# Two pairs of pieces share PSUM banks in a causal attention, and its plan is written in units

## The chip, the cores and the metric

The kernel runs on one core of a Trainium2 chip. The metric is the device time of one launch, in microseconds. It is given as the median of several runs; beside it there is one execution that was recorded by the hardware profiler, and all durations of single instructions come from that one. The core has five engines that run side by side and meet through semaphores: PE (matrix products, whose weight loads have a row of their own, PEld), DVE (vector work), ACT (activations and copies), POOL (more vector work) and SP (which issues DMAs). Products land in PSUM, which has eight banks of 128 partitions by 512 float32 numbers.

## The reference, cut to what matters

The whole program is two blocks of feed-forward, attention, feed-forward over x of 2 x 2048 tokens with 256 features, all in float32: first a mixture of experts around a full attention, then a gated recurrence around a causal attention. The change lies in the causal attention alone, which is this part of the reference:

```python
    x = x + _L1_attn_ref(_layernorm(x), w_q, w_k, w_v, w_o, rel_emb)

    # _L1_attn_ref, 16 heads of 16 features, L = 2048
    q = rotary(x @ w_q.T) / sqrt(16)
    k = rotary(x @ w_k.T)
    v = x @ w_v.T
    scores = einsum('bhqd,bhkd->bhqk', q, k)
    rel = rel_emb[clip(k_pos - q_pos, -32, 32) + 32]
    scores = where(causal, scores + einsum('bhqd,qkd->bhqk', q, rel), -1e18)
    attn = softmax(scores)
    ctx = einsum('bhqk,bhkd->bhqd', attn, v) + einsum('bhqk,qkd->bhqd', attn, rel)
    out = ctx @ w_o.T
```

The relative term differs from a constant only within 32 keys before the query. That strip, with the diagonal block of 128 keys, is the "band" of a query block: 160 columns.

## The kernel before

`attention1` works in 32 groups. A group is a batch b, a block of 512 queries (qc = 0 to 3) and four heads (g), whose four copies j = 0 to 3 sit in partitions 32j to 32j+31. A product with 32 rows uses only one quarter of PE's rows, so that the products of four heads can be in the array at once. I call these quadrant products. Transposes of bands, and most jobs, use the whole array; the products with the values (`weighted`, line 1231) use 128 rows and 32 columns, one quarter of the columns for each head.

Each group passes through two stages, which overlap with the neighbouring groups:

- **The maxima** (`largest`, line 1115). The queries come in four blocks of 128 (qb). For each query block there are the far pieces (up to 512 keys each, one product, one DVE maximum of 512 columns, line 1131) and one near piece: the band (160 columns, in one or two products) and the keys of the own block before the band (96, 224 or 352 columns for qb = 1, 2, 3). On a near piece DVE adds the band's relative scores and takes its maximum in one instruction (line 1147, followed by a small read of its accumulator), and for qb > 0 takes the maximum of the rest (line 1152). After the fourth head DVE makes the negated maximum (line 1157), and one unit later POOL adds it to the stored band (`later`, line 1161).
- **The exponentials** (`exp_band`, `exp_far`, `exp`, lines 1187 to 1229). For each block of 128 keys the scores come with keys as partitions, in one bank for each head: the bands are transposed into it (lines 1218 and 1222), the rest is a quadrant product (lines 1201 and 1208). ACT takes the exponential into `pT`. One unit later `weighted` multiplies with the values into one bank (line 1237), ACT copies that (line 644) and POOL adds it to the group's sum (line 542). The last two key blocks of a group, k0+2 and k0+3, have 256 and 128 query columns left; each takes four banks, four exponentials, four products with values, a copy and an add.

The order of all this is written out by a planner (lines 1270 to 1378). It has steps of two units; a unit has at most one piece of the maxima and one key block, and runs the bands' transposes, then the quadrant products of both (heads j and j+2 taken in turn), then `weighted` of the unit before, then jobs. For k0+3 the bands come after the maxima's products. A group has 2(qc+1) steps for either stage, `Ms` to `Me` for the maxima and `Es` to `Ee` for the exponentials; `Es` is two steps after `Me` or later. A group's maxima must also wait for one of three band tiles (`free`, from the group three before) and, on every second group, for the end of the group five before. The jobs (`at`) are all other things: keys and queries with their rotation (`rotate`), values, positions, `subtract` (which puts the maxima into the queries), `divide`, output products, and layer norms for later. The jobs of one step are dealt over its two units in halves. DMAs and copies that follow a job after some time have units of their own (`sends`).

All PSUM banks are one pool of eight that is used in turn (`bank`, line 73): a new bank is the one taken eight allocations before.

Of the kernel before, what the change touches and what calls it, by code (L numbers as in the profile page):

```python
# [42 lines left out]
def macaron_kernel(ctx: ExitStack, tc: tile.TileContext, t: dict, out: bass.AP):  # L43
# [935 lines left out]
    def attention1(norm, tail, w, relk, relv, kbias, dramp, skew):  # L979
# [4 lines left out]
        with ExitStack() as s:  # L984
# [24 lines left out]
            def rotate(xa, wa, b, qc, g):  # L1009
# [8 lines left out]
                if step < 0:  # L1018
                    nc.vector.tensor_tensor(xa, xa, cos[b, qc], ALU.mult)
                    nc.vector.tensor_tensor(xb, xb, sin[b, qc], ALU.mult)  # L1020
                    nc.vector.tensor_tensor(xa, xa, xb, ALU.add)
                else:
                    op = nc.gpsimd.tensor_tensor
                    z.later(1, op, xa, xa, cos[b, qc], ALU.mult)
                    z.later(2, op, xb, xb, sin[b, qc], ALU.mult)
                    z.later(3, op, xa, xa, xb, ALU.add)
# [80 lines left out]
            def pieces(qc):  # L1107


                far = [(qb, c) for c in range(qc) for qb in range(CPB)]  # L1110
                return far + [(qb, None) for qb in range(CPB)]
# [3 lines left out]
            def largest(t, qb, c, j):  # L1115
                b, qc, g = groups[t]
                i = qc * CPB + qb
                ps = bank()
                lhsT = q[t][rows(j), ts(qb, P)]
                m = mx[t][:, qb, j]  # L1120

                def product(cols, c, k0, n):
                    nc.tensor.matmul(  # L1123
                        ps[:, ds(cols, n)], lhsT=lhsT, rhs=kT[b, c, g][rows(j), ds(k0, n)],
                        start=True, stop=True,
                    )

                if c is not None:
                    n = min(TB, i * P - BAND - c * TB)
                    product(0, c, 0, n)  # L1130
                    nc.vector.tensor_reduce(m[:, c : c + 1], ps[:, 0:n], AX.X, ALU.max)  # L1131
                    return
                lo = 0
                if qb:
                    product(0, qc, qb * P - BAND, BW)
                    n = qb * P - BAND
                    product(BW, qc, 0, n)
                else:
                    if i:
                        product(0, qc - 1, TB - BAND, BAND)  # L1140
                    else:
                        lo = BAND
                        if j == 0:
                            nc.vector.memset(band[t][:, 0, :, 0:BAND], MASKED)
                    product(BAND, qc, 0, P)
                at_ = band[t][:, qb, j, lo:]
                nc.vector.tensor_tensor_reduce(  # L1147
                    out=at_, in0=ps[:, lo:BW], in1=at_, scale=1.0, scalar=3.0 * MASKED,
                    op0=ALU.add, op1=ALU.max, accum_out=m[:, qc : qc + 1],
                )  # L1150
                if qb:
                    nc.vector.tensor_reduce(m[:, qc + 1 : qc + 2], ps[:, ds(BW, n)], AX.X, ALU.max)
                done[t, qb] = done.get((t, qb), 0) + 1
                if done[t, qb] < J:
                    return
                mneg = z.mnegs[t % 2][:, qb]
                nc.vector.tensor_reduce(  # L1157
                    mneg[:, :, z.row(t)], mx[t][:, qb, :, 0 : qc + 1 + (qb > 0)], AX.X, ALU.max,
                    negate=True,
                )  # L1160
                z.later(
                    1, nc.gpsimd.tensor_tensor, band[t][:, qb], band[t][:, qb],
                    mneg[:, :, ds(z.row(t), 1)].to_broadcast([P, J, BW]), ALU.add,
                )
# [9 lines left out]
            def key_blocks(qc):  # L1174

                k0 = qc * CPB
                if qc == 0:
                    return [0, 1, 2, 3]
                far = list(range(k0 - 1))
                near = [k0, k0 + 1, k0 + 2, k0 - 1, k0 + 3]  # L1180
                order = []
                for k in near[:-1]:
                    order += [k] + far[:1]
                    far = far[1:]
                return order + near[-1:] + far

            def exp_bank(t, kb, j):
                if (t, kb, j) not in st:
                    st[t, kb, j] = bank()
                return st[t, kb, j]  # L1190

# [21 lines left out]
            def exp_band(t, kb, j):  # L1213
# [3 lines left out]
                if qb >= 0:  # L1217
                    nc.tensor.transpose(ps[:, ts(qb, P)], band[t][:, qb, j, BAND:], ident)  # L1218
# [7 lines left out]
            def exp(t, kb, j):  # L1226
                q0 = max(0, kb - groups[t][1] * CPB) * P
                z.pTs[t, kb, j] = wk.tile([P, TB], F32, name="pT", bufs=8)
                nc.scalar.activation(z.pTs[t, kb, j][:, q0:], st.pop((t, kb, j))[:, q0:], AF.Exp)  # L1229

            def weighted(t, kb):
                b, qc, g = groups[t]
                q0 = max(0, kb - qc * CPB) * P
                pv = bank()
                for j in range(J):
                    h = (g % 2) * J + j
                    nc.tensor.matmul(  # L1237
                        pv[rows(j), q0:],
                        lhsT=v[b, kb // CPB, g // 2][:, kb % CPB, ds(h * VW, 32)],
                        rhs=z.pTs.pop((t, kb, j))[:, q0:], start=True, stop=True,  # L1240
                    )
                z.gather(t, pv, 3, q0)
# [27 lines left out]
            Ms, Me, Es, Ee, Rs, By = ([] for _ in range(6))  # L1270
            for n, (b, qc, g) in enumerate(groups):
                size = 2 * (qc + 1)
                start = Me[-1] + 1 if n else 0
                free = Es[n - NBAND] + (4 if groups[n - NBAND][1] else 2) if n >= NBAND else -9
                start = max(start, free + 5 - size)
                if n > 5 and n % 2 == 0:
                    start = max(start, Ee[n - 5] + 5)
                Ms.append(start)
                Me.append(start + size - 1)
                By.append(max(free, start - 3))  # L1280
                start = Me[-1] + 2
# [4 lines left out]
                Rs.append(start + 5)  # L1286


            largest_at, exp_at, sends = Jobs(), Jobs(), Jobs()
            for n, (b, qc, g) in enumerate(groups):  # L1290
                for i, piece in enumerate(pieces(qc)):
                    largest_at.at(Ms[n] + i // 2, None, n, *piece)
                for i, kb in enumerate(key_blocks(qc)):
                    exp_at.at(Es[n] + i // 2, None, n, kb)
            jobs = Jobs()
            at = jobs.at
            index = {x_: n for n, x_ in enumerate(groups)}
            early = {
                n: max(Ms[n] - 10, Ee[n - 5] + 1) if n > 5 else Ms[n] - 8 for n in range(0, NG, 2)
            }  # L1300
            for n in range(NG):
                at(Me[n] + 1, z.subtract, n)
            for n in early:
                at(early[n], queries, n)
                sends.at(2 * early[n] + (2 if early[n] < 0 else 6), queries_out, n)
            for b in range(B):
                for qc in range(SB):
# [3 lines left out]
                    free = early[index[b, done_, G - 2]] + 2 if done_ is not None else f - 14  # L1311
                    at(max(f - 14, free), tables, b, qc)
                    if b or qc > 1:
                        for c in range(CPB):
                            at(f - 17 + c, z.ln_stats, b, qc, c)
                        at(f - 11, z.ln_transpose, b, qc)
                    for g in range(0, G, 2):
                        f = Ms[index[b, max(qc, 1), g]]
                        due = f - 7 if qc == 0 else f - 5 - (f < 6)
                        out_ = 2 * due + (2 if f < 6 else 6)  # L1320
                        free = 2 * Ee[index[b - 1, SB - 1, g + 1]] + 2 if b and qc else 2 * due
                        at(due, keys, b, qc, g, 2 * due < free)
                        sends.at(max(out_, free), keys_out, b, qc, g)
                    for half in range(2):
                        due = Es[index[b, max(qc, 1), 2 * half]] - 1 + (qc == 0)
                        at(due if b or qc > 1 or half else -2, vals, b, qc, half)
            for n, (b, qc, g) in enumerate(groups):
                e = early[n - n % 2]
                by = max(By[n], e + (3 if e < 0 else 4))
                at(by, by_position, n)  # L1330
                sends.at(max(2 * by + 3, 2 * (Ms[n] + 2 * qc) - 6), band_load, n)
                sends.at(2 * Me[n] + 4, band_store, n)
                sends.at(2 * Es[n] + 3, positions_load, n)
                sends.at(2 * Es[n] + 6, positions_exp, n)
                at(Rs[n] - 1, positions_T, n)
                at(Rs[n], positions, n)
                end = max(Rs[n], Ee[n] + 1)
                at(end + 1, z.divide, n, b, qc, g, False)
                if g == G - 1:
                    at(end + 2, z.outputs_T, b, qc)  # L1340
                    at(end + 3, z.outputs, b, qc, 0)
                    at(end + 4, z.outputs, b, qc, 1)

            for step, fn, *args in tail:
                at(Me[-1] + step, fn, *args)
            ready = []
            for step in range(min(jobs), max(jobs) + 1):
                exps = [a for _, a in exp_at.get(step, ())]
                maxs = [a for _, a in largest_at.get(step, ())]
                todo = jobs.get(step, [])  # L1350
                for n in range(2):
                    z.begin(2 * step + n)
                    sends.run(2 * step + n)
                    e = exps[n] if n < len(exps) else None
                    m = maxs[n] if n < len(maxs) else None
                    qb = e[1] - groups[e[0]][1] * CPB if e is not None else -2
                    if -1 <= qb < CPB - 1:
                        for j in range(J):
                            exp_band(*e, j)
# [242 lines left out]
```

## Time and profile before

| | |
|---|---|
| median of three runs | 4071.13 us (4068.05 to 4072.09) |
| the profiled execution | 4068.88 us, of which its span is 4067.0 us |
| mean granted PE clock | 0.993 |
| causal attention, first rotation to last output product | about 2578 to 3874 us of the span |
| PE busy in that stage (2700 to 3800 us) | 98% to 100% of each 100 us |
| DVE and ACT there | 62% to 77%, 58% to 76% |

The profiled time is the span and 1.9 us around it, and it lies 2.3 us under the median. A PE row is called busy from the first to the last of overlapping products, so the share says that PE seldom stood empty, not that it was used well. One product in float32 is two PE records, one transpose is one. A record's listed time holds the latency of the array; how fast records follow one another is read from their starts.

### The profile page before, as it was taken

Reading aid. Unit: us, or ns where it says so; the run is one execution under the profiler, and the core shown is the slowest. Engines: PE = TensorE matmul, PEld = TensorE weight load, DVE = VectorE, ACT = ScalarE, POOL = GpSimd, SP = SyncE. Lnnn points to the kernel's source line nnn. Section 1 sums busy time; section 2 is a strip of 40 time slices with the busy share of each in tenths; the row PEclk is TensorE's granted clock in tenths of the full one; section 3 lists DMA queues with packets and bytes.
Section 4 is the critical chain, followed back from the end, with each engine's and each line's share of the span. In section 5 each row is a group of like instructions: output and inputs, shape, how many; then the busy total and the mean of one; then the engine's idle time right before and its main releaser. Section 6 shows DMA issues by size and latency. Waiting matters only on the chain.

```text
span 4067.0 us, 76436 instructions
## 1 busy us (share of the span) xinstructions
PE 3996.5 (98%) x28256; PEld 1930.7 (47%) x28256; DVE 2701.9 (66%) x6128; ACT 2568.8 (63%) x5227; POOL 1634.8 (40%) x1456
## 2 busy tenths in 40 slices
PE   8999999999999999999999999999999999999999
PEld 4665333333344333333356655555554455554445
DVE  6247888888866888888752444667677766677533
ACT  2333788888887888888833322366667766667832
POOL 4245333336333333333442340345635645544410
PEclk9999999999999999999999999999999999999999
DMA  7341000100000000000033420334533344442101
GB/s 256 122 128 58 1 1 1 48 1 1 1 1 1 1 1 1 1 1 1 10 110 126 129 76 0 78 82 104 111 71 74 82 81 87 91 96 49 45 22 42
DMA packets 355508, 223.18 MB, mean 55 GB/s; under 512 B 146624, under 2 KB 338496, under 8 KB 355136
## 3 DMA queue, kind: packets, MB, share of 16 engines
q1 hardware_dynamic: 276800, 176.33, 16.5%
q0 software_dynamic: 12288, 33.57, 2.6%
q10 hardware_dynamic: 66048, 8.39, 1.3%
q8 instruction: 225, 3.69, 0.4%
q14 instruction: 147, 1.20, 0.1%
HBM read 113.12 MB, written 105.12 MB: 54 GB/s over the span
## 4 chain that ended last, share of the span: by engine, by line
PE 90%; DVE 5%; POOL 1%; ACT 1%; issue 1%; DMA 0%; SPq 0%; POOLq 0%; ACTq 0%; DVEq 0%
PE s L770 13%; PE s L782 12%; PE s L756 10%; PE s L146 10%; PE s L1237 7%; PE s L1123 6%; PE s L383 6%; PE s L1208 6%; PE s L403 3%; PE s L681 2%; PE s L1222 1%; PE s L1201 1%; PE s L1218 1%; PE s L344 1%; PE s L931 1%
## 5 line engine op out<-in xcount | busy, mean ns | idle before, releaser
L542 POOL TENSOR_TENSOR part<-part 128x512 f32<-128x512 f32 (+3 forms) x800 | 962.0, 1203 | 1389.9 <-ACT part L644 1377.0
L760 DVE TENSOR_REDUCE mx<-s 128x1 f32<-128x512 f32 x2048 | 1271.0, 684 | 292.8 <-PE s L756 292.6
L775 ACT ACTIVATE pT<-s 128x512 f32<-128x512 f32 x2048 | 1063.6, 618 | 200.7 <-PE s L756 199.1
L756 PE MATMUL s<-kT,q 32*128 32x512 f32 x4096 | 1018.6, 618 | 1.9 <-DVE mx L760 1.9
L770 PE MATMUL s<-q,kT 32*128 32x512 f32 x4096 | 1013.0, 615 | 0.4 <-DVE q L639 0.4
L1229 ACT ACTIVATE pT<-s 128x512 f32<-128x512 f32 (+3 forms) x1280 | 587.8, 542 | 252.8 <-PE s L1208 102.0
L770 PEld LDWEIGHTS s<-q,kT 32*128 32x128 f32 x4096 | 417.8, 183 | 466.9 <-DVE mx L760 327.0
L644 ACT COPY part<-s 128x512 f32<-128x512 f32 (+3 forms) x864 | 508.2, 589 | 148.2 <-PE s L782 60.2
L1131 DVE TENSOR_REDUCE mx<-s 128x1 f32<-128x512 f32 (+1 forms) x768 | 473.0, 679 | 132.3 <-PE s L1123 123.9
L782 PE MATMUL s<-pT,v 128*32 128x512 f32 x4096 | 549.8, 605 | 0.6 <-ACT pT L775 0.2
L756 PEld LDWEIGHTS s<-kT,q 32*128 32x128 f32 x4096 | 406.4, 184 | 128.9 <-ACT pT L775 76.2
L1123 PE MATMUL s<-kT,q 32*128 32x512 f32 (+7 forms) x2240 | 332.1, 433 | 0.0
L1237 PE MATMUL s<-pT,v 128*32 128x512 f32 (+3 forms) x2560 | 304.7, 541 | 9.1 <-DVE mx L1131 5.0
L383 PE MATMUL s<-we,xT 128*128 x592 | 278.7, 593 | 0.2 <-ACT xT L378 0.2
L390 DVE TENSOR_TENSOR h<-sg,s 128x256 f32<-128x256 f32 x148 | 62.4, 422 | 289.5 <-ACT sg L388 289.3
L1123 PE MATMUL s<-b,q 32*128 32x512 f32 (+7 forms) x1280 | 243.0, 518 | 1.6 <-DVE v L612 1.4
L782 PEld LDWEIGHTS s<-pT,v 128*32 128x32 f32 x4096 | 82.1, 108 | 336.1 <-ACT pT L775 300.4
L1147 DVE CUSTOM_DVE_ANT_0 band<-s,band 128x160 f32<-128x160 f32 (+1 forms) x512 | 155.7, 314 | 127.2 <-PE s L1208 62.6
L542 POOL TENSOR_TENSOR band<-band,mneg 128x640 f32<-128x640 f32 x128 | 161.3, 1260 | 189.2 <-DVE mneg L1157 127.9
L1208 PE MATMUL s<-q,kT 32*128 32x512 f32 (+3 forms) x1152 | 236.3, 509 | 0.0
L436 POOL DMA_INDIRECT yg<-results,at x128 | 123.8, 967 | 235.0 <-DMA results<-y 197.6
L1208 PE MATMUL s<-q,b 32*128 32x512 f32 (+3 forms) x896 | 208.5, 568 | 0.0
(227 smaller groups left out, 5148.1 us busy)
## 6 DMA issues: line engine op xcount, KB each, us to landing
band<-skew SPq DMA_DIRECT2D x32, 1280.0 KB, 7.5
pd<-band SPq DMA_DIRECT2D x32, 1280.0 KB, 8.5
xs<-places SPq DMA_DIRECT2D x148, 128.0 KB, 2.2
results<-y SPq DMA_DIRECT2D x148, 128.0 KB, 1.7
places<-zero SPq DMA_DIRECT2D x2, 4736.0 KB, 16.4
we<-in_we SPq DMA_DIRECT2D x12, 768.0 KB, 11.6
skew<-s ACTq DMA_DIRECT2D x32, 256.0 KB, 3.0
s<-pd SPq DMA_DIRECT2D x32, 256.0 KB, 4.3
```

The lines of the kernel that those rows point to most:

```text
L383: nc.tensor.matmul(pu, lhsT=xT[n][:, ts(kc, P)], rhs=w[:, kc, ds(val[n], 2 * D)], start=kc == 0, stop=kc == 1,)
L542: fn(*args)
L644: nc.scalar.copy(part[:, q0:], pv[:, q0:])
L756: nc.tensor.matmul(ps, lhsT=q[t][rows(j), ts(qb, P)], rhs=kT[b, g][rows(j), ts(kc, TB)], start=True, stop=True,)
L760: nc.vector.tensor_reduce(mx[t][:, qb * J + j, kc : kc + 1], ps, AX.X, ALU.max)
L770: nc.tensor.matmul(st, lhsT=kT[b, g][rows(j), ts(kb, P)], rhs=q[t][rows(j), :], start=True, stop=True,)
L775: nc.scalar.activation(z.pTs[t, kb, j], st, AF.Exp)
L782: nc.tensor.matmul(pv[rows(j), :], lhsT=v[b, g // 2][:, kb, ds(h * VW, 32)], rhs=z.pTs.pop((t, kb, j)), start=True, stop=True,)
L1123: nc.tensor.matmul(ps[:, ds(cols, n)], lhsT=lhsT, rhs=kT[b, c, g][rows(j), ds(k0, n)], start=True, stop=True,)
L1208: nc.tensor.matmul(ps[:, q0:], lhsT=k, rhs=q[t][rows(j), q0:], start=True, stop=True, skip_group_check=True,)
L1229: nc.scalar.activation(z.pTs[t, kb, j][:, q0:], st.pop((t, kb, j))[:, q0:], AF.Exp)
L1237: nc.tensor.matmul(pv[rows(j), q0:], lhsT=v[b, kb // CPB, g // 2][:, kb % CPB, ds(h * VW, 32)], rhs=z.pTs.pop((t, kb, j))[:, q0:], start=T ...
```

## The change

The four main edits, all inside `attention1`:

1. The near pieces of qb = 0 and qb = 1 are one piece `(0, 1)` in one bank (columns 0 to 159 and 160 to 415). The same four products and the same three DVE instructions for each head are issued, all products first.
2. The last two key blocks are one entry `(k0+2, k0+3)`. k0+3's 128 columns go to columns 128 to 255 of k0+2's bank, so there is one exponential of 384 columns for each head; `weighted` adds both key blocks up in one bank, with one copy and one add for both. Its twelve transposes come ahead of the products, as for the other bands.
3. The order of the near key blocks is k0, k0+1, k0-1, last pair, each followed by a far one while there are any.
4. The plan counts in units. A group has 4 qc + 3 units for either stage, in place of 4 qc + 4. All distances are restated in units. A job that would stand one unit early, where the next unit has no bands but the one after has, is put off by one unit (`at`), so that it runs straight in front of bands. `subtract` is not put off.

`rotate` now asks whether the unit, not the step, is below zero before it lets DVE do the rotation.

```diff
-                if step < 0:
+                if z.unit < 0:
...
-                far = [(qb, c) for c in range(qc) for qb in range(CPB)]
-                return far + [(qb, None) for qb in range(CPB)]
+                far = [((qb,), c) for c in range(qc) for qb in range(CPB)]
+                return far + [((0, 1), None), ((2,), None), ((3,), None)]
...
+                for qb in qbs:
+                    at_, n, lo = qb * BW if len(qbs) > 1 else 0, max(0, qb * P - BAND), 0
+                    if qb:
+                        product(qb, at_, qc, qb * P - BAND, BW)
+                        product(qb, at_ + BW, qc, 0, n)
...
+                        product(qb, at_ + BAND, qc, 0, P)
+                for qb in qbs:
...
+                    nc.vector.tensor_tensor_reduce(
+                        out=c_, in0=ps[:, at_ + lo : at_ + BW], in1=c_, scale=1.0,
...
                 k0 = qc * CPB
+                last = (k0 + 2, k0 + 3)
                 if qc == 0:
-                    return [0, 1, 2, 3]
+                    return [(0,), (1,), last]
                 far = list(range(k0 - 1))
-                near = [k0, k0 + 1, k0 + 2, k0 - 1, k0 + 3]
                 order = []
-                for k in near[:-1]:
-                    order += [k] + far[:1]
+                for k in ((k0,), (k0 + 1,), (k0 - 1,), last):
+                    order += [k] + [(f,) for f in far[:1]]
                     far = far[1:]
...
             def exp_bank(t, kb, j):
+                kb -= kb - groups[t][1] * CPB == CPB - 1
...
+                    h, pT = (g % 2) * J + j, z.pTs.pop((t, kbs, j))
+                    for kb in kbs:
+                        q0, c0 = max(0, kb - qc * CPB) * P, exp_cols(qc, kb)
+                        nc.tensor.matmul(
+                            pv[rows(j), q0:],
...
+                            rhs=pT[:, ds(c0, TB - q0)], start=kb == kbs[0],
+                            stop=kb == kbs[-1], skip_group_check=len(kbs) > 1,
+                        )
+                z.gather(t, pv, 3, max(0, kbs[0] - qc * CPB) * P)
...
-                size = 2 * (qc + 1)
+                size = CPB * qc + 3
                 start = Me[-1] + 1 if n else 0
-                free = Es[n - NBAND] + (4 if groups[n - NBAND][1] else 2) if n >= NBAND else -9
-                start = max(start, free + 5 - size)
+                free = Es[n - NBAND] + (8 if groups[n - NBAND][1] else 4) if n >= NBAND else -18
+                start = max(start, free + 9 - size)
...
+            def bands(unit):
+                n, kbs = exp_at.get(unit, (0, (-9,)))
+                return kbs[0] - groups[n][1] * CPB >= -1
+
+            def at(unit, fn, *args):
+
+                jobs.at(unit + (not bands(unit + 1) and bands(unit + 2)), fn, *args)
...
+                if e is not None:
+                    n, kbs = e
+                    if bands(unit):
+                        for kb in kbs:
+                            for j in range(J):
+                                exp_band(n, kb, j)
+                for j in range(J):
+                    if e is not None:
+                        for kb in kbs:
+                            exp_far(n, kb, j)
+                        exp(n, kbs, j)
+                    if m is not None:
+                        largest(*m, (j + 2) % J if e is not None else j)
+
+
+                for a_ in ready:
+                    weighted(*a_)
+                ready = [e] if e is not None else []
+                jobs.run(unit)
```

## The prediction

> **What bounds the kernel now.** I read the page first, then the stage's busy time in windows, then its groups of instructions by shape, and last the timeline of PE for single units.
>
> ```profile
> PE 3996.5 (98%) x28256; PEld 1930.7 (47%) x28256; DVE 2701.9 (66%) x6128; ACT 2568.8 (63%) x5227; POOL 1634.8 (40%) x1456
> ...
> PE 90%; DVE 5%; POOL 1%; ACT 1%; issue 1%; DMA 0%; SPq 0%; POOLq 0%; ACTq 0%; DVEq 0%
> ```
>
> 90% of the chain that ended last is PE. The windows say the same of the causal stage (columns: busy us of PE, PEld, DVE, ACT, POOL, then clock and DMA):
>
> ```profile
> 3300.00:3400.00 100.00, 99.33 (x925) 54.71 (x924) 65.22 (x180) 64.38 (x140) 44.41 (x40) 1.00 0.42 83
> ```
>
> The other engines have a quarter to a third of their time free, POOL more, and the clock is full. What the change edits on DVE are these groups of the stage (count, then busy us and mean ns):
>
> ```profile
> L1131 DVE TENSOR_REDUCE mx<-s 128x1 f32<-128x512 f32 x672 | 416.6, 683 | 112.5 <-PE s L1123 112.1
> L1147 DVE CUSTOM_DVE_ANT_0 band<-s,band 128x160 f32<-128x160 f32 x480 | 148.1, 317 | 122.1 <-PE s L1123 62.6 <-PE s L1208 57.5
> ...
> L1147 DVE DVE_READ_ACCUMULATOR2_ANT mx<- 128x1 f32 x512 | 42.4, 83 | 0.0
> L1152 DVE TENSOR_REDUCE mx<-s 128x1 f32<-128x96 f32 x128 | 32.3, 253 | 0.0
> ```
>
> Then PE's timeline, where the edges between kinds of work can be read:
>
> ```profile
> 3302.78 0.66 PE L1259 MATMUL s<-ident,s 128*128 128x128 f32 x4
> 3303.27 1.06 PE L1083 MATMUL s<-relk,q 128*128 128x128 f32 x8
> 3304.17 0.27 PE L1218 MATMUL s<-ident,band 128*128 128x128 f32 x1
> ...
> 3304.93 0.27 PE L1222 MATMUL s<-ident,band 128*128 128x128 f32 x1
> 3305.13 0.34 PE L1201 MATMUL s<-q,kT 32*96 32x128 f32 x1
> ...
> 3307.08 1.06 PE L1237 MATMUL s<-pT,v 128*32 128x512 f32 x8
> 3308.07 1.13 PE L1264 MATMUL s<-s,relv 128*128 128x512 f32 x2
> 3309.13 0.69 PE L1208 MATMUL s<-q,b 32*128 32x512 f32 x1
> ```
>
> A transpose follows the last in 0.109 us, and four 512-column records in four quadrants go through in 0.43 us. So eight of `weighted` should need 0.85 us, but the next work starts after 0.99 (3307.08 to 3308.07): an edge of 0.14. Two whole-array records of 512 (0.85) need 1.06: 0.2. From the last band at 3304.93 to the first quadrant product are 0.20, of which 0.11 is streaming. I cut the whole stage in this way into stretches of quadrant, value and whole-array work. Between the first and the last unit with exponentials they take 1244.4 us, of which some 990 is streaming. The remainder is edges, quadrants that do not overlap, and waits. The change can only act on these, since the streamed records stay the same.
>
> **Edges of whole-array stretches.** The median edge is 0.160 us after jobs alone, 0.169 after bands alone, 0.231 after jobs and bands together, and 0.406 where k0+3's four transposes stand between the maxima and `weighted` (next timeline, 2794.02 to 2794.78: 0.76 for 0.43 of streaming). Writing out both plans gives, before, 145, 63, 57 and 32 of them: 23.2 + 10.6 + 13.2 + 13.0 = 60.0 us. After, 73, 34, 85 and 0: 11.7 + 5.7 + 19.6 = 37.0 us. Saved: **23.0 us**.
>
> **Value stretches.** 32 fewer (319 to 287), each with an edge of 0.143: **4.6 us**. The pair's sixteen records stream the same columns. Four of one quarter now come in a row; in the quadrant work four in a row (3305.13, two L1201 and two L1208 for a head) let the next head start 0.02 us later, so I add nothing.
>
> **Quadrant stretches.** Their number falls from 330 to 310. At the median of each shape the 330 are 561.9 us. Of the 310, 258 have a shape that occurs before (446.6 us), 21 lie between two such shapes (40.3 us), and 31 hold the new pair (0, 1), which no row shows. Its nearest row is a piece of 160 + 96 columns beside far exponentials:
>
> ```profile
> 2790.12 0.69 PE L1208 MATMUL s<-q,b 32*128 32x512 f32 x1
> 2790.13 0.40 PE L1123 MATMUL s<-kT,q 32*128 32x160 f32 x1
> 2790.14 0.69 PE L1208 MATMUL s<-q,b 32*128 32x512 f32 x1
> 2790.15 0.73 PE L1123 MATMUL s<-kT,q 32*128 32x160 f32 x7
> 2790.66 0.66 PE L1208 MATMUL s<-q,b 32*128 32x512 f32 x3
> 2791.09 0.29 PE L1123 MATMUL s<-kT,q 32*128 32x160 f32 x1
> 2791.09 0.69 PE L1208 MATMUL s<-q,b 32*128 32x512 f32 x1
> ...
> 2792.14 1.06 PE L1237 MATMUL s<-pT,v 128*32 128x512 f32 x8
> 2793.14 0.95 PE L1123 MATMUL s<-kT,q 32*128 32x160 f32 x16
> 2794.02 0.66 PE L1218 MATMUL s<-ident,band 128*128 128x128 f32 x4
> 2794.78 1.07 PE L1237 MATMUL s<-pT,v 128*32 128x512 f32 x8
> ```
>
> It takes 2.02 us (2790.12 to 2792.14), as much as the piece of 32 + 128 beside such exponentials. The fourth head's exponential product starts at 2791.09 only, when the head queued ahead of it starts, though its own quadrant had ended the near products at about 2790.9. So a head with many short records holds up those behind it. In one quadrant a record follows another in 0.109 us up to 128 columns, in 0.136 at 160: eight records of the pair are 6 x 0.109 + 2 x 0.136 = 0.93 us. The lower bound is 2.02 us (all four heads side by side, hidden under the exponentials). The upper is 2.8: three heads held for about 0.55 us each (somewhat over half a run of 0.93), then the last one's 0.93 and an edge of 0.2. I take 2.6, nearer the upper, as that row shows the hold. Eight of the 31 (qc = 0, without the 32-column product) I put at 2.2. The mean is 2.5, and 31 x 2.5 = 77.5. Together 446.6 + 40.3 + 77.5 = 564.4 us: **2.5 us more** than before. Bounds: 15 less (31 x 0.48) to 9 more (31 x 0.3) than that.
>
> The Trainium skill, "TensorE: Matmul & The Clock Gate" (Part 3: Packing small matmuls), has two rules that disagree here: that weight loads for another row group are pulled ahead of products in flight, and that products start and end in strict order. By the first the pair would stand at its lower bound; by the second, four heads in series, it would be at 3.7 us or more and that term alone would use up the savings on edges. The row above shows something between: the second head does start ahead of the first's later records, the fourth does not.
>
> **Waits.** Before, the stage lasts 1244.4 us for 1202.6 priced, so 41.8 us are waits. DVE's work for the pair is 8 x (0.317 + 0.083) + 4 x 0.253 + 2 x 0.17 = 4.55 us in one unit, where PE has 2.6 + 1.0. The near units of a group hold 4.55 + 3.31 + 3.85 = 11.7 us of DVE in three units in place of four, against 9.65 us on PE without jobs. With eight banks a unit's last piece is wanted about 2.7 us after its product ended. Letting DVE fall that far behind PE and counting the excess as waits, unit by unit, gives 8.5 us before and 14.2 after; ACT by the same count gives 6.0 and 9.5. Part of it is that fewer units hold both stages: in mid-stage 22 have maxima alone (12 before) and 14 exponentials alone (4 before), since the short groups of qc = 0 now wait for band tiles. I add **9 us**; bounds none and, as that count sees only a third of the 41.8, 26.
>
> **Edits at nothing.** ACT loses 128 exponentials of 0.289 us, gains 0.105 on 128 others, and loses 32 copies of 0.291; POOL loses 32 adds. Neither bounds the stage, so none of it is counted; if ACT's lateness makes most of the waits, it is worth a few us. DMAs are the same. A put-off rotation moves its three POOL operations by one unit and its copies into heads (`sends`) not: two units of slack remain. A put-off job that waits for DMA or POOL holds PE's bands behind it; the jobs already stood there, so no price. Start: one more rotation runs on DVE, 0.73 + 3 x 0.69 = 2.8 us, ahead of the first maxima, partly in place of a later one: **2 us**.
>
> **Sum.** -23.0 - 4.6 + 2.5 + 9 + 2 = -14 us: 4055 in the terms of the profiled 4068.9, and 4057 beside the median of 4071.1. About 0.2%, 8 us, is what a measurement of this kernel can tell from no change.
>
> **Rivals.**
> - *DVE and the banks become the bound (slower).* Jobs now gather in front of exponential bands, so the three near units of maxima may have none beside them; then the excess of 11.7 - 9.65 = 2.05 us comes in full as PE waiting for a bank. In two thirds of the groups that is 42 us, and the sum is -25 + 2 + 42 = +19: 4090. It decides from 1 us of new waits for each group on. For it: 4.55 us in one unit; against it: DVE is only 65% busy, and the near units of before show few waits.
> - *Nothing to see.* The pairs cost 2.8 each and waits grow by 14 us: -25 + 9 + 14 + 2 = 0: 4071.
> - *More than forecast.* Quadrants overlap freely and ACT's lighter load offsets DVE's: -25 - 15 + 2: 4033.
> - *The plan does not do what it says.* The count of jobs joined to bands (57 to 85) speaks against it; under 0.02, left in the second.
>
> **How the numbers follow.** Forecast (4045 to 4063) 0.40, more 0.10, nothing to see (4063 to 4079) 0.26, slower 0.24. That is 0.50 faster, 0.26 the same, 0.24 slower. The range takes the lower bounds in, to 4033, and reaches to 4088 in the slower case; about 0.1 lies above.
>
> **What would show it.** Right: streamed PE records unchanged; no edges of 0.4 us ahead of `weighted`; stretches with the pair of 2.2 to 2.8 us; DVE idle before L1131 smaller; about 23 units fewer. Wrong: pairs over 3 us, or PE's weight loads waiting for DVE after pairs by 1 us a group, or short groups leaving PE waiting at their bands.

## The result, and the profile after

The changed kernel takes 4049.25 us (median of six runs, 4045.64 to 4050.07) beside 4069.84 us for the kernel before (4067.27 to 4072.09) on the same chip: a ratio of 0.995, with a 95% interval of 0.994 to 0.996. That is 20.6 us less. The profiled execution took 4049.04 us with a span of 4047.2, which is 19.8 us less than the span before.

The page's lines on the engines and on the chain that ended last, of the changed kernel:

```profile
PE 3983.2 (98%) x28256; PEld 1968.7 (49%) x28256; DVE 2700.0 (67%) x6131; ACT 2554.4 (63%) x5067; POOL 1617.6 (40%) x1421
...
PE 91%; DVE 4%; ACT 1%; POOL 1%; issue 1%; DMA 0%; SPq 0%; POOLq 0%; ACTq 0%; DVEq 0%
```

PE has the same 28256 records and still carries the chain; its busy time fell by 13.3 us. ACT has 160 instructions less and POOL 35 less. Three of DVE's six thousand are new: the rotation that moved to DVE at the start. The window of mid-stage (columns: busy us of PE, PEld, DVE, ACT, POOL, then clock and DMA) shows no other engine near its limit:

```profile
3300.00:3400.00 100.00, 100.00 (x951) 59.82 (x953) 68.65 (x185) 63.25 (x125) 43.88 (x38) 1.00 0.40 80
```

PE ran 951 records in these 100 us, for 925 before, though not the same ones. DVE's groups by shape (count, busy us and mean ns, then the idle time just before them and what ended it):

```profile
L1129 DVE TENSOR_REDUCE mx<-s 128x1 f32<-128x512 f32 x672 | 416.0, 682 | 129.1 <-PE s L1120 128.8
L1150 DVE CUSTOM_DVE_ANT_0 band<-s,band 128x160 f32<-128x160 f32 x480 | 146.7, 317 | 80.4 <-PE s L1120 61.1 <-PE s L1221 19.1
...
L1150 DVE DVE_READ_ACCUMULATOR2_ANT mx<- 128x1 f32 x512 | 42.5, 83 | 0.0
L1156 DVE TENSOR_REDUCE mx<-s 128x1 f32<-128x96 f32 x128 | 32.5, 254 | 0.2
```

The work is the same. DVE's idle time ahead of near pieces fell from 122.1 to 80.4 us, while that ahead of far pieces grew from 112.5 to 129.1. A DVE that had become the bound would have lost both.

For the rest I cut the stage into stretches by the starts of PE's records, as the prediction did, for every kernel. "Start" is from the first rotation product to the first band transpose of a unit with exponentials; "middle" goes on to the last such unit; the total goes to the last whole-array product. All in us:

| | start | middle | of it whole-array | quadrant | value | total |
|---|---|---|---|---|---|---|
| before | 42.2 | 1244.4 | 376.6 in 297 stretches | 587.6 in 330 | 280.2 in 319 | 1291.3 |
| after | 47.8 | 1218.9 | 346.5 in 193 | 597.5 in 310 | 274.9 in 287 | 1271.4 |

The total fell by 19.9, all of the gain in the span. Of the whole-array stretches 72.8 us were not streaming before, and 44.3 are not now. The kind with transposes between the maxima and `weighted` is gone. What the pair costs is read from PE's timeline of one unit that holds it (start us, listed us, instruction, shape, count):

```profile
3055.66 0.69 PE L1221 MATMUL s<-q,kT 32*128 32x512 f32 x1
3055.67 0.71 PE L1120 MATMUL s<-kT,q 32*128 32x32 f32 x4
...
3056.22 0.30 PE L1120 MATMUL s<-kT,q 32*128 32x160 f32 x1
3056.22 0.69 PE L1221 MATMUL s<-q,kT 32*128 32x512 f32 x1
3056.23 0.71 PE L1120 MATMUL s<-kT,q 32*128 32x32 f32 x7
3056.75 0.59 PE L1221 MATMUL s<-q,kT 32*128 32x512 f32 x1
3056.78 0.30 PE L1120 MATMUL s<-kT,q 32*128 32x160 f32 x1
3056.78 0.69 PE L1221 MATMUL s<-q,kT 32*128 32x512 f32 x1
...
3057.34 0.30 PE L1120 MATMUL s<-kT,q 32*128 32x160 f32 x1
3057.34 0.69 PE L1221 MATMUL s<-q,kT 32*128 32x512 f32 x1
3057.35 0.71 PE L1120 MATMUL s<-kT,q 32*128 32x32 f32 x7
...
3058.45 1.07 PE L1254 MATMUL s<-pT,v 128*32 128x512 f32 x8
```

The four heads' exponential products begin at 3055.66, 3056.22, 3056.78 and 3057.34: each 0.56 us after the last (3056.75 is the second record of the head before). As far as the quadrants go, which are four different ones, they could have started together. Each time the next head's first product starts at the moment (3056.22, 3056.78, 3057.34) when the head ahead starts its first record of 160 columns, the fifth of its eight. `weighted` follows at 3058.45, so the unit's quadrant stretch is 2.79 us. The two pairs that have no exponentials beside them (at 2996.19 and 3621.97) take 2.77 us, so the exponentials have no part in this length.

### The profile page after: what moved, and what is told of

Same layout as the page of the kernel before. It is cut to its first block, busy times and chain, and to the rows that moved or that the text cites. A ratio compares the mean times of both kernels' runs of the same rounds, so it can differ in the third digit from the quotient of the medians.

```text
span 4047.2 us, 76303 instructions
## 1 busy us (share of the span) xinstructions
PE 3983.2 (98%) x28256; PEld 1968.7 (49%) x28256; DVE 2700.0 (67%) x6131; ACT 2554.4 (63%) x5067; POOL 1617.6 (40%) x1421
## 4 chain that ended last, share of the span: by engine, by line
PE 91%; DVE 4%; ACT 1%; POOL 1%; issue 1%; DMA 0%; SPq 0%; POOLq 0%; ACTq 0%; DVEq 0%
PE s L770 13%; PE s L782 12%; PE s L756 10%; PE s L146 9%; PE s L1120 7%; PE s L1254 7%; PE s L383 6%; PE s L1221 6%; PE s L403 3%; PE s L1231 2%; PE s L681 1%; PE s L1214 1%; PE s L1237 1%; PE s L604 1%; PE s L344 1%
## 5 line engine op out<-in xcount | busy, mean ns | idle before, releaser
L542 POOL TENSOR_TENSOR part<-part 128x512 f32<-128x512 f32 (+2 forms) x768 | 947.9, 1235 | 1402.0 <-ACT part L644 1398.2
L1245 ACT ACTIVATE pT<-s 128x512 f32<-128x512 f32 (+1 forms) x1152 | 580.5, 585 | 207.4 <-PE s L1221 101.4
L644 ACT COPY part<-s 128x512 f32<-128x512 f32 (+2 forms) x832 | 500.1, 602 | 162.9 <-PE s L782 60.2
L1120 PE MATMUL s<-kT,q 32*128 32x160 f32 (+6 forms) x2240 | 342.2, 429 | 0.0
L1120 PE MATMUL s<-b,q 32*128 32x512 f32 (+7 forms) x1280 | 260.7, 516 | 0.7 <-DVE mx L1129 0.7
```

What stands on the lines that cost most here:

```text
L542: fn(*args)
L644: nc.scalar.copy(part[:, q0:], pv[:, q0:])
L1120: nc.tensor.matmul(ps[:, ds(cols, n)], lhsT=q[t][rows(j), ts(qb, P)], rhs=kT[b, c, g][rows(j), ds(k0, n)], start=True, stop=True,)
L1245: nc.scalar.activation(z.pTs[t, kbs, j][:, q0:], ps[:, q0:], AF.Exp)
```

## Experiments

My theory (A in the expectations) was that the gain comes from fewer and shorter edges of PE, that the pair costs what its timeline shows because a head with eight short records holds those behind it, and that DVE is no bound. The rivals put the gain, or the loss inside it, on the order of the jobs, on the banks, or on DVE. Four kernels (jobs in place, first pieces apart, all apart, the pair in rounds) ran where the kernel before took 4069.29 us; the others where everything ahead of the stage took some 130 us more, so that the kernel before took 4202.67 us, and 4202.25 for the last two. So ratios to the kernel before and durations of the stage are compared, not times. Three chips were used: one for the first four, one for the next four, and one for the last two. The changed kernel itself ran once more, as the last one: its stage is 1269.4 us, 2.0 less than above. The clock can account for most of that. In the middle of the trace above the granted clock was 0.5 for 6.8 us (3010.5 to 3013.9 and 3624.9 to 3628.3), in this one for 3.4 us (3144.8 to 3148.2); where it was 0.5, as at 2620 us before the change, transposes started every 0.21 us in place of 0.109. The other traces have between none and 11 us of it in the middle. So a difference of 2 or 3 us between two traces is not told from the clock.

**Jobs in place.** A job is not put off by a unit.

```diff
-                jobs.at(unit + (not bands(unit + 1) and bands(unit + 2)), fn, *args)
+                jobs.at(unit, fn, *args)
```

> The changed kernel, with the put-off of jobs taken out: a job runs in the unit it is due in, also where the next unit has no bands. Theory A (the gain is PE's edges between kinds of work, which fall mostly because a unit's jobs are no longer dealt over two units and because k0+3's bands no longer stand between the maxima and the values): the plan then has 91 stretches of jobs alone, 42 of bands alone and 77 of both, against 73, 34 and 85; at the edges of 0.160, 0.169 and 0.231 us that is 2.4 us more, so 1 to 5 us slower than the changed kernel, about 4052. Rival (the jobs put in front of bands are what pays): most of the 23 us on edges comes back, 4060 or more.

Measured: 4050.25 us, ratio 0.9953 (0.994 to 0.9967), the stage 1271.7 us. That is 0.3 more in the stage than with the change. Putting jobs in front of bands joins 8 more of them (85 for 77 stretches) and is worth nothing that can be measured. Most of the joins are there without it: 211 whole-array stretches against 297 before and 193 with the change, since a step's jobs are no longer dealt over two units.

**First pieces apart.** (0, 1) is two pieces again, with units of their own; the rest stays.

```diff
-                return far + [((0, 1), None), ((2,), None), ((3,), None)]
+                return far + [((qb,), None) for qb in range(CPB)]
...
-                size = CPB * qc + 3
+                size = CPB * qc + 4
...
-                Ee.append(start + size - 1)
+                Ee.append(start + size - 2)
```

> The changed kernel, with the first two near pieces apart again (a group's maxima take 4 qc + 4 units, its exponentials 4 qc + 3). Theory A: the pair holds PE for 2.8 us, two stretches of one piece each 2.02 beside exponentials that are wanted anyway; pricing the plan stretch by stretch gives 1174 us against 1176, so within 4 us of the changed kernel, 4045 to 4053. Rival B (fewer units are what pays): half of the gain goes with half of the removed units, 4058 or more. Rival C (DVE's 4.5 us in one unit makes PE wait): faster than the changed kernel by over 6 us.

Measured: 4051.05 us, 0.995 (0.9937 to 0.9964), the stage 1271.6. The pair of first pieces gains nothing: its units saved are paid back by stretches of 2.8 us and by a longer start (47.8 us with it, 43.0 without).

**All apart.** As the last, and k0+2 and k0+3 are two entries again, with k0+3's bands still ahead of the products.

```diff
-                last = (k0 + 2, k0 + 3)
+                last = (k0 + 2,)
...
-                    return [(0,), (1,), last]
+                    return [(0,), (1,), last, (3,)]
...
-                for k in ((k0,), (k0 + 1,), (k0 - 1,), last):
+                for k in ((k0,), (k0 + 1,), (k0 - 1,), last, (k0 + 3,)):
```

> The changed kernel with neither pair: pieces apart and the last two key blocks apart (each with its own banks, exponentials, copy and add), 4 qc + 4 units for both stages, in the order k0, k0+1, k0-1, k0+2, k0+3. What is left of the change is the plan in units, all bands ahead of the products, and the jobs in front of bands. Theory A: edges of 86.8 us priced, against 78.1 in the changed kernel and 105.6 before, all stretches 1180 against 1176 and 1198: 4050 to 4057. Rival B (sharing is what pays: fewer units, 160 fewer ACT instructions, 32 fewer adds): back at 4066 to 4074.

Measured: 4056.88 us, 0.997 (0.9958 to 0.9982), the stage 1277.9. Without any shared bank 12.4 of the 20.6 us remain (7 to 17 by the interval), so by the medians most of the gain has nothing to do with the banks. Sharing the last two key blocks is worth 6.3 us of the stage (1277.9 to 1271.6).

**The last band behind.** As "all apart", with k0+3's transposes after the maxima, as in the kernel before.

```diff
+                    end = kbs[0] - groups[n][1] * CPB == CPB - 1
-                    if bands(unit):
+                    if bands(unit) and not end:
...
+                if e is not None and end:
+                    for j in range(J):
+                        exp_band(n, kbs[0], j)
+                        exp(n, kbs, j)
```

> The run with all apart, and in it the bands of k0+3 stand behind the unit's maxima, as they did before the change. Theory A: 32 edges of 0.406 us come back, others go; priced 95.3 us of edges against 86.8, so 6 to 11 us slower than with all apart, 4063 to 4068. Rival (where the bands stand costs nothing; the gain of that run is the jobs no longer dealt over two units): within 3 us of it, 4054 to 4060.

Measured: ratio 0.9979 (0.9971 to 0.9988), the stage 1280.5 us. Against "all apart" (1277.9; 0.997) that is 2.6 us by the trace and about 4 by the ratios, under the 6 to 11 of my theory. The 2.6 us lie within the rival's 3, the intervals of the two ratios overlap, and the two kernels ran on different chips, so the times do not decide between the two. The edges came back as priced, 56.6 us beside 46.1, in 221 stretches; but the quadrant stretches fell from 601.9 to 593.4 when the maxima's products come first. So by these two traces moving the transposes ahead of the products saves 10.5 us of edges and gives 8.5 back. That DVE gets its work sooner with the maxima in front would explain it; no run separates that from the rest.

**The pair in rounds.** The pair's four heads issue their qb = 0 products in the usual order, and their qb = 1 products, with the DVE work, after all four.

```diff
-                for qb in qbs:
+                for qb in qbs if len(qbs) == 1 else qbs[second : second + 1]:
...
+                if len(qbs) > 1 and not second:
+                    halves[t, j] = ps
+                    return
...
+                if m is not None:
+                    for j in range(J):
+                        largest(*m, (j + 2) % J if e is not None else j, True)
```

> The changed kernel, with the pair's products issued in two rounds over the heads: first the products of query block 0 for all four heads among the exponentials, then those of query block 1 for all four, so that no head has eight short records in a row; the DVE work follows the second round. Theory A (heads queued behind a head with many short records are held): stretches with the pair go from 2.8 us to 2.0 to 2.3, 31 of them, 15 to 25 us faster than the changed kernel: 4024 to 4034. Rival (the quadrants were busy all that time, no hold): no change, 4046 to 4052. Rival C (DVE is what sets the near units): the stretches get shorter, but PE's waits grow by as much, 4043 or more.

Measured: 4045.58 us, 0.9941 (0.9928 to 0.9955), the stage 1266.4. The 31 pair stretches fell from 85.6 to 69.4 us, as a hold by a long run of records wants it. But only 5 of these 16.2 us arrived, about what rival C expected, and by the ratios even these are not told from nothing (the changed kernel has 0.994 to 0.996). Up to 3.4 of the 5 can be the clock, as this trace has none of the 6.8 us at 0.5 that the changed kernel's has. The windows of one pair unit and the one behind it tell where the rest went. First the changed kernel (columns as above):

```profile
2906.80:2910.60 3.80, 3.80 (x50) 2.86 (x48) 2.49 (x19) 1.99 (x5) 0.84 (x1) 1.00 0.02 4
2910.60:2914.10 3.50, 3.50 (x46) 2.38 (x43) 2.78 (x16) 2.88 (x6) 3.45 (x3) 1.00 0.00 0
```

Then the pair in rounds, where the pair's values end at about 2910.60 too:

```profile
2908.20:2910.60 2.40, 2.40 (x49) 1.51 (x48) 0.98 (x8) 1.64 (x4) 0.77 (x1) 1.00 0.00 0
2910.60:2914.10 3.50, 3.50 (x44) 2.55 (x40) 3.43 (x25) 2.65 (x5) 1.91 (x2) 1.00 0.02 5
```

In the first kernel DVE does 2.49 us of its work while the pair and the values behind it run. In the second it gets 0.98 done there and is busy for 3.43 of the 3.50 us that follow, and PE now waits for it: that unit's quadrant stretch grew from 2.02 to 2.77 us, and over all groups the unit behind the pair went from 58.3 to 68.6 us, the next from 59.9 to 63.3. DVE's timeline shows why it starts so late, and how fast it then goes (the bracket is the idle time before, and what ended it):

```profile
2909.62 0.33 DVE L1157 CUSTOM_DVE_ANT_0 band<-s,band 128x160 f32<-128x160 f32 x1 [2.79 <-PE s L1124]
2909.87 0.08 DVE L1157 DVE_READ_ACCUMULATOR2_ANT mx<- 128x1 f32 x1
2909.87 0.32 DVE L1157 CUSTOM_DVE_ANT_0 band<-s,band 128x160 f32<-128x160 f32 x1
2910.11 0.08 DVE L1157 DVE_READ_ACCUMULATOR2_ANT mx<- 128x1 f32 x1
2910.11 0.25 DVE L1163 TENSOR_REDUCE mx<-s 128x1 f32<-128x96 f32 x1
2910.28 0.31 DVE L1157 CUSTOM_DVE_ANT_0 band<-s,band 128x160 f32<-128x160 f32 x1
...
2910.94 0.31 DVE L1157 CUSTOM_DVE_ANT_0 band<-s,band 128x160 f32<-128x160 f32 x1
...
2911.59 0.31 DVE L1157 CUSTOM_DVE_ANT_0 band<-s,band 128x160 f32<-128x160 f32 x1
```

It stood idle for 2.79 us until the first head had both halves. After that a head's five instructions take 0.66 us (2909.62, 2910.28, 2910.94, 2911.59), although their listed durations add up to 1.06.

**The pair by two heads.** The second halves follow after each two heads, so that DVE starts sooner.

```diff
+                    if m is not None and j % 2:
+                        for i in (j - 1, j):
+                            largest(*m, (i + 2) % J if e is not None else i, True)
```

> As the pair in rounds, but two heads at a time: query block 0's products of two heads among the exponentials, then query block 1's of these two, then the same for the other two. No head has more than four records in a row, and DVE gets the first head about 0.3 to 0.4 us sooner than in the run with four heads at a time, where the unit after a pair gave back 0.5 to 0.8 us. Theory A (the give-back is DVE's late start): pairs of 1.5 to 2.3 us and a give-back smaller by the 0.3 to 0.4 us in some 25 units, 5 to 10 us faster than that run, 4036 to 4041. Rival (DVE's rate over the pair's unit and the next sets the time): as that run, 4042 to 4049.

Measured: ratio 0.9913 (0.99 to 0.9926), the stage 1257.7 us. The pairs take 68.5 us, no more than in rounds, and the units behind them 61.7 and 61.8: of the 13.7 us given back, 5.3 are left. In the unit that answers to the one above, DVE's first work stands 0.83 us ahead of the pair's end (3039.88 and 3040.71), in rounds 0.03 (2909.62 and 2909.65), and the unit behind takes 2.25 us in place of 2.77. The stage is 11.7 us shorter than that of the changed kernel in its second run, on another chip of the same speed, and the intervals of the two ratios do not meet (0.99 to 0.9926 and 0.9942 to 0.997). So the pair's size is set by the run of short records in one quadrant, and the next unit by when DVE gets its first work.

**Near pieces among far ones.** As the last, with the pair and the piece of qb = 2 each followed by a far piece, in groups that have enough of them; their band is loaded two units earlier.

```diff
+                return far[:-2] + near[:1] + far[-2:-1] + near[1:2] + far[-1:] + near[2:]
```

> As the pair by two heads, and for groups of qc = 2 and 3 the near pieces stand among the far ones: pair, far, third, far, fourth, with the last two far pieces in between. Theory A (DVE falls behind over the run of near pieces and PE pays right after): the far units, where DVE needs less than PE, take the lateness up, 4 to 10 us faster than the pair by two heads. Rival (the lateness only moves, or is not DVE's): within 3 us of it.

Measured: ratio 0.9913 (0.99 to 0.9926), the stage 1255.7. The 2.0 us in the trace do not show in the ratio, and both lie in the rival's range. Spreading DVE's load over more units is worth little.

**The start.** The third group's queries, and what follows from them, come two units later, so that one rotation fewer runs on DVE before the first unit.

```diff
-                n: max(Ms[n] - 20, Ee[n - 5] + 2) if n > 5 else Ms[n] - 16
+                n: max(Ms[n] - 20, Ee[n - 5] + 2) if n > 5 else Ms[n] - 16 + 2 * (n == 2)
```

> The changed kernel, with the rotation of the third group's queries two units later, so that it falls in unit 0 and POOL does it, as before the change. The stage's first exponential stood at 2626.2 us with the change and 2619.9 before. Theory A (DVE's extra rotation ahead of the first maxima delays them): 3 to 6 us of these 6.3 come back, 4043 to 4047. Rival (the start hangs on other waits: DMA, other rotations): within 2 us of the changed kernel.

Measured: ratio 0.9935 (0.9922 to 0.9947), the stage 1267.7 us, of which the start is 45.0. Beside the second run of the changed kernel (1269.4, start 47.4) it gains 1.7 us by the trace; by time it is not told from nothing, as the intervals overlap. That is the rival's range. The two points in the expectation are unlike: 2619.9 is the first transpose before, 2626.2 the first quadrant product after, whose transposes begin at 2625.3.

**What helped, together,** and the changed kernel again for comparison: near pieces among far ones, the pair by two heads, and the start.

> The pair by two heads, the near pieces among the far ones, and the third group's rotation left to POOL, together. From the first rotation to the last product with the stage's own durations: 1271.4 us in the changed kernel, 13.7 less with the pair by two heads, 2.0 less again with near among far, 3.7 less with the start alone. Theory A (the three act in different places): 17 to 20 us faster than the changed kernel, if both run on the same chip. Rival (the start's gain and the near pieces' lie on the same wait): 13 to 16 us.

> The changed kernel itself, beside the run above on the same chip, since two sets of runs were on chips of different speed. Expected 0.994 to 0.996 of the kernel before, as measured at first.

Measured: 4165.22 us (4159.93 to 4169.1) and 0.9915 (0.9902 to 0.9929) for the first; 4180.64 us and 0.9956 (0.9942 to 0.997) for the second. The stages are 1250.1 and 1269.4 us. So a version that is some 15 us faster than the change exists, which is the rival's 13 to 16 and not my 17 to 20. From the pair by two heads alone (0.9913) it is not told apart. In its timeline of PE the four heads of a pair, no longer in one run of eight, overlap:

```profile
3168.39 0.69 PE L1231 MATMUL s<-q,kT 32*128 32x512 f32 x1
3168.39 0.29 PE L1127 MATMUL s<-kT,q 32*128 32x32 f32 x1
3168.41 0.69 PE L1231 MATMUL s<-q,kT 32*128 32x512 f32 x1
...
3168.92 0.61 PE L1231 MATMUL s<-q,kT 32*128 32x512 f32 x2
3168.94 0.74 PE L1127 MATMUL s<-kT,q 32*128 32x160 f32 x11
3169.41 0.62 PE L1231 MATMUL s<-q,kT 32*128 32x512 f32 x1
...
3169.52 0.62 PE L1231 MATMUL s<-q,kT 32*128 32x512 f32 x1
...
3170.49 1.06 PE L1264 MATMUL s<-pT,v 128*32 128x512 f32 x8
```

Two heads start together at 3168.39 and 3168.41, the other two only at 3169.41 and 3169.52, behind the short records of the first two, and the stretch ends after 2.10 us (3168.39 to 3170.49).

## Why the prediction was right or wrong

The forecast was 4057 us, the measurement 4049.25: faster, as forecast, and by some 7 us more (20.6 beside 14). That it came so near is luck in part: the pair and the start were sized too low and the waits too high, and these errors cancel. Term by term, in us of the stage:

| term | forecast | measured | from |
|---|---|---|---|
| edges of whole-array stretches | -23.0 | -23.0 | the planned counts at the same median edges |
| value stretches | -4.6 | -4.6 | 287 for 319 |
| quadrant stretches, all pairs as long as they were | +2.5 | +10.0 | 31 pairs take 85.6, not 77.5 |
| waits | +9 | -6.2 | 1218.9 less 1183.3 priced, beside 41.8 before |
| start | +2 | +5.6 | 47.8 for 42.2 |
| streamed jobs that moved into the start | not counted | -1.7 | 302.1 for 303.8 |
| sum | -14 | -19.9 | |

The first two rows are counts at the medians of before, and the waits are what is left over. The times themselves changed by -30.1 us in whole-array stretches, +9.9 in quadrant ones, -5.3 in value ones and +5.6 in the start.

**Edges and values** held. The steps that counted them from both plans and priced them by the medians of the trace of before needed no correction: the whole-array excess fell by 28.5 (72.8 to 44.3), which covers the 23.0; the other 5.5 are booked as waits that lay in these stretches, which no run separates. But the experiments divide this gain otherwise than the change's title. Reading the totals as a ladder: 1291.3 before; 1280.5 with the plan in units and its order of key blocks (up to 2 more of it may be the chip's); 1277.9 with k0+3's transposes ahead; 1271.6 with the last two key blocks shared; 1271.4 with the first pieces shared too. Putting jobs in front of bands is worth 0.3 of it. Each step holds to 2 or 3 us only, for the clock and the chips, so the last one and the 0.3 are not told from nothing.

**The pair** was sized too low, though the mechanism was read rightly. I took 2.6 us for a pair with far exponentials, between 2.02 and 2.8. Undisturbed ones are 2.77 to 2.82: the hold of about 0.55 us for each head that stood in the text as the upper bound was measured at 0.56. That it fits so well is luck: the row that I used has four records for each head, not eight, and its second head starts 0.02 us after the first, so "somewhat over half a run" was a guess that no row showed. Eight pairs of qc = 0 were put at 2.2; four take 2.24 and four 3.06. The trace shows what holds the four: ACT first does an instruction of 512 columns on keys (L139, 2814.62 to 2815.43), which the other four do not have beside them, and then the exponentials of the unit before; these end at 2815.81, 2816.19, 2816.57 and 2816.95, and 0.05 us after each of them a product of the pair starts (2815.86, 2816.24, 2816.62, 2817.00), waiting on ACT's semaphore. It is the same in all four. So 4 x 0.82 = 3.3 us of the +10.0 are waits for ACT, and the pairs themselves made it some +6.7. The two rules of the Trainium skill, "TensorE: Matmul & The Clock Gate" (Part 3: Packing small matmuls), weight loads pulled ahead for other row groups and products in strict order, would have given 2.02 and 3.7 by the prediction's working; the pair shows neither. The next head starts before the last one's records are through, but not before they are about half through.

**Waits** were the step that failed most, by 15 us and with the wrong sign (by 12, with the 3.3 us of those four pairs counted here). It rested on DVE's load: 4.55 us of DVE work in a unit where PE has 2.6 + 1.0. That figure is a sum of listed durations, and these overlap: a head of the pair takes 0.66 us on DVE when it runs without waiting, so four take 4 x 0.66 + 0.3 = 2.9 us, and the pair's 2.8 us on PE hide it. The waits in quadrant stretches stayed as they were (25.7 us before and after); those elsewhere fell from 16.1 to 9.8, most of it in whole-array stretches. The rise that I had counted from listed durations (5.7 us for DVE, 3.5 for ACT) did not come, but for the four pairs that wait for ACT. The slower rival (DVE and the banks) falls with the same figure: no pair outside qc = 0 shows a wait (all 23 take 2.77 to 2.82 us). Its mechanism is real, as the pair in rounds shows, but it needs DVE's first work to be late, not much.

**The start** was forecast at a third of its size. I priced the rotation on DVE (2.8 us) and took some of it as saved later. Of the 5.6 us 1.5 stand ahead of the first product of the maxima (13.4 us after the first rotation product, 11.9 before), the rest behind it; 1.7 us are job records that the middle no longer has. The start grows only where the first pieces share (43.0 us in "first pieces apart"), as the shorter groups bring one more rotation below unit zero. That this rotation makes the growth is shown in part: with it back on POOL the first maxima come after 11.9 us again, but the start is 45.0 in "the start" and 43.2 in the run with all that helped. It is not the clock: in the changed kernel's two traces the start has some 17 and 10 us at a granted clock of 0.5 and takes 47.8 and 47.4.

What the text named as signs came out so: records unchanged; no more edges of 0.4 us ahead of `weighted`; 23 units fewer (319 for 342 by the two plans); pairs of 2.24 to 2.82 us, but for the four over 3, which were named as a sign of being wrong; no wait for DVE after pairs. One did not: DVE's idle time before far pieces grew, and so was no sign against the change.

What remains open: what else lengthens the start, and whether the change's fewer waits in whole-array stretches come from the smaller number of these stretches or from ACT's lighter work. The profile names ACT and DVE in turn as the releasers there, and no run separated them.

## What to carry to other kernels

Price a merge by the longest run of short records that it puts behind one another in one part of the array, not by its sum of columns: here two pieces merged into one gained nothing until their records were dealt out again by two heads, and then the same merge was worth some 12 us. When a stretch of the bound engine is shortened, look at once at when its consumer gets its first work; a shorter stretch that starts the next engine later is paid back in the next unit. Find out whether an engine's listed durations overlap before adding them up to a load.

## What the runs showed of the hardware

- Eight float32 records in one quadrant (0.91 us from the first start to the last) hold the products of the next head, in another quadrant, for 0.56 us, until the fifth of them starts. With four in a row, as in the last timeline, the next head starts after 0.02 us.
- DVE's near-piece instructions of one head, 0.33, 0.08, 0.32, 0.08 and 0.25 us as listed, follow one another within 0.66 us: from the first of them to the third are 0.25 us (0.41 listed for the two between), from the last to the next head's first 0.17 (0.25 listed).
- Transposes ahead of a unit's quadrant products instead of behind them saved 10.5 us of edges on PE in 32 units, and the quadrant stretches grew by 8.5 (one trace of each, on two chips).
